# Two transformer layers with routed experts on one core: the order in which group two's shared expert, the layer-1 weights, gathers, sends and the mixing are issued

## The chip, the core and the metric

The kernel runs on one core of a Trainium2 chip. The metric is device time in microseconds (us) of that core. The kernel before was timed in three runs, and its median is what a change is compared with. One further execution was profiled; its times are those of every line of profile in this document.

## What is computed

The input is 8 sequences of 256 tokens with 256 channels, in 32-bit floats. Four blocks follow each other, each on a layer-normed copy of x and each added to x:

```
x = x + attention0(norm(x))      # q, k and v from one projection; softmax over rows plus softmax over columns
x = x + ffn0(norm(x))            # 4 experts, top 2 of them, plus one shared expert for every token
x = x + mixing1(norm(x))         # time mixing: a recurrence over the tokens of a sequence
x = x + ffn1(norm(x))            # 8 experts, top 2 of them
```

ffn0 runs, for every token, silu(x·w1)·(x·w3)·w2 of its two best experts, weighted with their softmax probabilities, and the same form with the shared weights sw1, sw3, sw2. mixing1 projects three mixtures of each token and the one before it to k, v and r, runs an exponentially decaying weighted mean of v with stabilised exponents, layer-norms it, gates it with r and projects it back. ffn1 computes silu-like gates with biases, a product, and a second projection with a bias.

## The kernel before, in words

The sequences are called b0 to b7 here. A sequence lies on the chip as one tile `xs[b]` of 128 partitions by 2 by 256. They are split into two groups, b0 to b4 and b5 to b7 (`GROUPS`, L32). Each group passes each feed-forward block as one `Experts` object (L673): `one` and `two` are the groups of ffn0, `three` and `four` those of ffn1. Such an object works in steps that are Python generators:

- `choose` and `route` (L729, L755): some 35 small VectorE operations that pick two experts per token and give each token two slots in a list that is sorted by expert and padded to blocks of 128 rows.
- `sends` (L806): GpSimd writes the normed rows into a DRAM list `sent` with indirect DMAs, 128 rows each: 20 for a group of five sequences, 12 for a group of three.
- `tiles` (L869): for each block of 128 rows, SyncE's queue fetches the rows (`xg`, L884) and for layer 1 the expert's bias (L883). TensorE turns them (L891), multiplies (L899), turns the hidden values (L891 on `h`) and multiplies again. SyncE stores the result in `back` (L929). There are 23, 15, 27 and 19 tiles in `one`, `two`, `three` and `four`. A fetch waits for every send of its group.
- `shared` (L826): for layer 0 the shared expert of each sequence (matmuls L855, a product on VectorE L860, matmuls L863, an addition to x L866). For layer 1 it adds only the experts' second biases, by the small matmuls L844 and L848.
- `combine` (L948): for each sequence four indirect gathers from `back` on GpSimd (L957), and then four VectorE operations that add them to x (L965).

The time mixing (L980) has ten stages for a sequence, which come in steps of a generator, several sequences at once and four steps apart (`steps`, L1133): norm, mix (transposes L218 of `xr`, then VectorE L1019), project (24 matmul pieces, L1030), exponents, denominator, invert (L1077), numerator, norm_inner (transposes L1096), gate (transposes of `z`, then VectorE L1120) and project_out (L1127). Then come the layer-1 norm (`xm`), its transposes and the router's matmuls (L720). The mixing of b5 starts 8 steps late, since it needs x after `two.combine`.

The order on each engine is made in two layers. By hand, `weave` (L41) interleaves the generators in the given proportions, and `issue_after` ties tile steps behind matmuls of the mixing (`behind`, L1263). A list scheduler then orders the instructions of each engine by priority; a block under `high_priority(offset=...)` (L1151) stands ahead of its place in the program by that many instructions, as far as its inputs allow. Engines run their own queue in order. An instruction that waits holds up all behind it on that engine, on SyncE's and GpSimd's DMA queues too.

The layer-1 weights (`weights_1`, L1191: 24 loads of 256 KB on SyncE's queue) are given the memory that layer 0's weights and tile buffers occupied, so their loads wait for the last matmul that reads these. In the kernel before that is the last L863 of `two.shared`.

The order around the change is: `two.tiles` and then `two.shared` together with the mixing; `three.sends` with the last of them; `two.combine`; then the weights, `three.shared`, and `three.tiles` with the rest of the mixing; then `four`.

Of the kernel before, what the change touches and what calls it, by code (L numbers as in the profile page):

```python
# [12 lines left out]
ALU = mybir.AluOpType  # L13
# [11 lines left out]
E2, I2 = 8, 256  # L25
# [15 lines left out]
def weave(*streams):  # L41

    streams = [[g, n, 0] for g, n in streams]
    while streams:
        s = min(streams, key=lambda s: s[2] / s[1])
        s[2] += 1
        try:
            next(s[0])
        except StopIteration:
            streams.remove(s)  # L50


def one_by_one(*gens):
    for g in gens:
        yield from g


def take(gen, n):
    for _ in range(n):
        try:  # L60
            next(gen)
        except StopIteration:
            return
        yield
# [3 lines left out]
def two_layers(  # L68
# [26 lines left out]
    nc = tc.nc  # L95
# [10 lines left out]
    back = [dram.tile([n, D], F32, tag=f"back{k}", name=f"back{k}") for k, n in enumerate(slots_of)]  # L106
# [566 lines left out]
    class Experts:  # L673
# [195 lines left out]
        def tiles(self):  # L869

            mp, ps, mm, n_tiles, whose = self.mp, self.tile_ps, self.mm, self.n_tiles, self.whose
            xgs, xgTs, hs, hTs, experts, biases = {}, {}, {}, {}, {}, {}

            def fetch(j):
                xgs[j] = mp.tile([P, D], F32, tag="xg", name="xg", bufs=4)
                if self.layer:
                    e = nc.sync.value_load(whose[0:1, j : j + 1], min_val=0, max_val=self.n_experts - 1)  # L880
                    biases[j] = mp.tile([P, 2 * I2], F32, tag="bias", name="bias", bufs=4)
                    row = self.weights[2][ds(e, 1)].rearrange("e g d -> (e g d)")
                    nc.sync.dma_start(out=biases[j], in_=row.partition_broadcast(P))  # L883
                inst = nc.sync.dma_start(out=xgs[j], in_=self.sent[ts(j, P), :]).ins  # L884
                for name in self.senders:
                    tc.add_manual_dep(inst, name, landed, reason="any send may have rows of the tile")

            def flip(src, n, tag):
                pt = ps([P, n, P])
                for c in range(n):  # L890
                    nc.tensor.transpose(pt[:, c, :], src[:, ts(c, P)], ident)  # L891
                to = mp.tile([P, n, P], F32, tag=tag, name=tag)
                nc.scalar.copy(to, pt)  # L893
                return to

            def times(lhsT, w, e, n, cols):
                po = mm([P, cols])
                for c in range(n):
                    nc.tensor.matmul(  # L899
                        po.unsqueeze(1), lhsT=lhsT[:, c, :], rhs=w[:, ds(e, 1), c, :], start=(c == 0), stop=(c == n - 1)  # L900
                    )
                return po

            def up(j):
                at = whose[0:1, j : j + 1]
                e = experts[j] = nc.tensor.value_load(at, min_val=0, max_val=self.n_experts - 1)
                xgT = xgTs.pop(j)
                if self.layer:
                    ph = times(xgT, self.weights[0], e, NC, 2 * I2)
                    hb = mp.tile([P, 2 * I2], F32, tag="hb", name="hb")  # L910
                    nc.vector.tensor_tensor(hb, ph, biases.pop(j), ALU.add)  # L911
                    s = hs[j] = mp.tile([P, I2], F32, tag="h", name="h", bufs=3)
                    nc.scalar.activation(s, hb[:, 0:I2], AF.Silu, scale=ALPHA)
                    (nc.vector if self.last else nc.gpsimd).tensor_tensor(s, s, hb[:, I2:], ALU.mult)  # L914
                else:
                    pu = times(xgT, self.weights[0], e, NC, H1)
                    s = hs[j] = mp.tile([P, H1], F32, tag="h", name="h", bufs=3)
                    nc.scalar.activation(s, pu, AF.Silu)
                    pg = times(xgT, self.weights[2], e, NC, H1)
                    nc.vector.tensor_tensor(s, s, pg, ALU.mult)  # L920

            def down(j):
                py = times(hTs.pop(j), self.weights[1], experts.pop(j), n_hidden, D)
                yg = mp.tile([P, D], F32, tag="yg", name="yg", bufs=3)
                if self.layer:
                    nc.vector.tensor_copy(yg, py)
                else:
                    nc.scalar.copy(yg, py)  # L928
                nc.sync.dma_start(out=self.back[ts(j, P), :], in_=yg)  # L929

            n_hidden = (H1, I2)[self.layer] // P
            for j in range(3):
                fetch(j)
            xgTs[0] = flip(xgs.pop(0), NC, "xgT")
            for j in range(n_tiles + 2):
                if j + 3 < n_tiles:
                    fetch(j + 3)
                if j + 1 < n_tiles:
                    xgTs[j + 1] = flip(xgs.pop(j + 1), NC, "xgT")
                if j < n_tiles:  # L940
                    up(j)
                if 1 <= j <= n_tiles:
                    hTs[j - 1] = flip(hs.pop(j - 1), n_hidden, "hT")
                if j >= 2:
                    down(j - 2)
                yield
# [33 lines left out]
    def time_mixing(rp, rp1, wkv_w, ps, on_pe):  # L980
# [152 lines left out]
        def steps(seqs, first, after):  # L1133

            late = {}
            for b in seqs:
                m = after[b]  # L1140
                stages = [norm, mix, project, exponents, denominator, invert, numerator, norm_inner, gate, project_out]
                for k, f in enumerate(stages):
                    late.setdefault(first[b] + k, []).append((-k, f, b))

                for k, f in enumerate((m.norm, m.flip, m.judge)):
                    late.setdefault(first[b] + len(stages) - 1 + k, []).append((1.5 - len(stages) - k, f, b))
                if b == m.seqs[-1]:
                    late[first[b] + len(stages) + 1].append((1, lambda b, m=m: (m.choose(), m.route()), b))
            for n in range(max(late) + 1):

                with tc.high_priority(offset=3000):  # L1151
                    for _, f, b in sorted(late.get(n, []), key=lambda x: x[0]):
                        f(b)
                yield
# [45 lines left out]
    def layers(is_bounded):  # L1200
# [4 lines left out]
        with ExitStack() as pctx, ExitStack() as ctx0, ExitStack() as actx:  # L1205
# [14 lines left out]
            one, two = (Experts(0, k, w0, lnp, mp, rt, ps, mm, ps) for k in range(2))  # L1220
            group_of = {b: m for m in (one, two) for b in m.seqs}
            with ExitStack() as p1:
                psum.update(pool=p1.enter_context(tc.tile_pool(name="p1", bufs=1, space=PSUM)), ps=4, sc=4)
                if is_bounded:
# [3 lines left out]
                    steps = attention_bounded(ap1, ap2, ep, lambda: (ps, sc))  # L1228
# [20 lines left out]
            yp = pctx.enter_context(tc.tile_pool(name="y", bufs=2))  # L1249
# [7 lines left out]
            three, four = (Experts(1, k, None, lnp, None, rt, sc, mm, ps) for k in range(2))  # L1257
# [3 lines left out]
            mixing = time_mixing(rp, rw, wkv_w, sc, on_pe)(range(B), first, group_of)  # L1261

            def behind(gen, lag=1):  # L1263

                while True:
                    with tc.issue_after(on_pe[-lag].ins):
                        try:
                            next(gen)
                        except StopIteration:
                            return  # L1270
                    yield

            tiles = one_by_one(two.tiles(), two.shared())
            back = one.combine(yp)
            weave((take(back, 2), 2), (take(tiles, 1), 1))
            weave((back, 4), (take(mixing, 3), 3), (take(tiles, 3), 3))
            weave((take(mixing, 25), 25), (take(behind(tiles), 12), 12))
            assert three.chosen
            weave((three.sends(), 10), (behind(tiles), 4))
            weave((two.combine(yp), 4))  # L1280
            ctx0.close()

            wp = pctx.enter_context(tc.tile_pool(name="w2p", bufs=1, side="right"))
# [1 line left out]
            mp = pctx.enter_context(tc.tile_pool(name="moe1", bufs=2, side="right"))  # L1285
            for m in (three, four):
                m.weights, m.mp = w1_, mp
            weave((three.shared(), 5), (take(mixing, 4), 4))
            tiles = three.tiles()
            weave((take(behind(tiles, 3), 22), 22), (mixing, 16))  # L1290
            assert four.chosen
            weave((four.sends(), 6), (four.shared(), 3), (tiles, 7))
            weave((three.combine(yp), 6), (four.tiles(), 21))
            weave((four.combine(yp), 4))

# [14 lines left out]
    with tc.If(is_flat > 0) as which:  # L1310
        layers(True)
    with which.Else():
        attention_any()
        layers(False)
# [61 lines left out]
```

## Time and profile before

| what | value |
|---|---|
| median of 3 runs | 896.68 us (894.17 to 899.22) |
| the profiled execution | 877.61 us |
| its span, first to last instruction | 875.8 us |
| TensorE matmul busy (PE) | 703.4 us, 80% |
| weight loads (PEld) | 442.8 us, 51% |
| VectorE (DVE) | 452.6 us, 52% |
| ScalarE (ACT) | 362.3 us, 41% |
| GpSimd (POOL) | 235.9 us, 27% |
| mean granted TensorE clock | 0.909 |

In the trace the stages lie so: attention up to about 213 us, `one` from there to 376, the tiles of `two` with the mixing of b0 to b4 up to 558, a passage with few matmuls up to the first layer-1 tile at 641.6, then the tiles of `three` with the mixing of b5 to b7, from 777 those of `four`, and after the last matmul at 850 the last combine and the stores of the output.

How to read the views: a line of the timeline has the start in us, the length in us, engine, source line, operation, output<-inputs, shapes, and in square brackets how long the engine had been idle and who released it. A line of the waits has the total of the waits in us, their number and the longest. A line of the table of stretches has the stretch, its length, TensorE's busy time with its number of instructions, the granted clock as a share of full speed, the busy share of the DMA engines, and GB/s.

### The profile page before, as it was taken

The page shows a single profiled execution, that of the slowest core. Times are in us where ns is not written, and L with a number is a line of the kernel's source. Part 1 is how long each engine was busy: PE and PEld are TensorE (multiplying, and loading weights), DVE is VectorE, ACT ScalarE, POOL GpSimd, SP SyncE. Part 2 cuts the span into 40 slices and gives each one's busy share as a digit, 9 for nine tenths or more (in the row PEclk, how much of TensorE's full clock was granted, in tenths as well). Part 3 has the DMA queues.
Part 4 walks back from the last instruction along what each step waited for, and adds up shares of the span by engine and source line. Part 5 has one row for each costly group of instructions (what it writes and reads, how often), then busy time and mean ns, then how long its engine had stood idle before and what let it go on. Part 6 is the DMA issues. An engine that isn't in the chain of part 4 may idle for free.

```text
span 875.8 us, 11122 instructions
## 1 busy us (share of the span) xinstructions
PE 703.4 (80%) x3248; PEld 442.8 (51%) x3248; DVE 452.6 (52%) x1139; ACT 362.3 (41%) x781; POOL 235.9 (27%) x322
## 2 busy tenths in 40 slices
PE   2699888886999999967888889826767887986970
PEld 1354444444756666635565565714535554543640
DVE  4598876881411011126887666405686662345442
ACT  1486766751223333225656663301457342321320
POOL 3634332345320000045010101374012235235004
PEclk9799998987999999998999899965688999998995
DMA  7940000014111111132000000137502345557623
GB/s 237 337 151 1 1 1 1 1 42 152 55 55 49 49 48 37 43 103 67 25 19 25 15 10 19 55 102 246 169 19 78 97 138 163 164 147 220 185 80 110
DMA packets 62307, 76.94 MB, mean 88 GB/s; under 512 B 8184, under 2 KB 50208, under 8 KB 62240
## 3 DMA queue, kind: packets, MB, share of 16 engines
q1 hardware_dynamic: 54560, 58.76, 21.4%
q0 software_dynamic: 6144, 16.79, 6.1%
q10 hardware_dynamic: 1536, 0.60, 0.3%
q8 instruction: 31, 0.51, 0.2%
q14 instruction: 36, 0.29, 0.1%
HBM read 48.57 MB, written 27.54 MB: 87 GB/s over the span
## 4 chain that ended last, share of the span: by engine, by line
PE 46%; DVE 19%; POOL 15%; ACT 8%; issue 6%; DMA 5%; POOLq 0%; DVEq 0%; SPq 0%; ACTq 0%
PE mm L899 24%; POOL rr L473 4%; POOL y L957 4%; PE ps L891 4%; POOL sent L815 4%; PE sc L1030 4%; DMA y<-back,slot 2%; DVE s L535 2%; POOL rs L189 2%; PE sc L521 2%; DVE den L1077 1%; PE mm L848 1%; PE mm L863 1%; PE sc L1127 1%; PE mm L855 1%
## 5 line engine op out<-in xcount | busy, mean ns | idle before, releaser
L957 POOL DMA_INDIRECT y<-back,slot x64 | 62.4, 975 | 206.8 <-PE mm L899 133.5
L899 PE MATMUL mm<-v1s,xgT 128*128 x184 | 91.8, 616 | 1.7 <-ACT xgT L893 1.7
L920 DVE TENSOR_TENSOR h<-h,mm 128x512 f32<-128x512 f32 x38 | 26.1, 686 | 118.4 <-PE mm L899 118.4
L893 ACT COPY hT<-ps 128x256 f32<-128x256 f32 (+1 forms) x84 | 39.3, 468 | 115.8 <-PE ps L891 115.4
L815 POOL DMA_INDIRECT sent<-xm,slot x64 | 62.4, 975 | 56.5 <-DVE pick L787 38.7
L899 PE MATMUL mm<-w2s,hT 128*128 x304 | 73.5, 383 | 1.5 <-ACT yg L928 1.5
L899 PE MATMUL mm<-w3s,xgT 128*128 x152 | 73.3, 605 | 0.0
L899 PE MATMUL mm<-w1s,xgT 128*128 x152 | 72.3, 597 | 0.9 <-issue 0.6
L534 ACT ACTIVATE e<-sc,minus 128x512 f32<-128x512 f32 x96 | 59.7, 705 | 25.8 <-PE sc L521 25.8
L535 DVE TENSOR_REDUCE s<-e 128x2 f32<-128x512 f32 x96 | 60.2, 676 | 12.3 <-ACT e L534 11.9
L188 POOL TENSOR_TENSOR rs<-mv,eps_ln 128x2 f32<-128x2 f32 x40 | 9.1, 228 | 210.6 <-DVE mv L183 112.0
L473 POOL TENSOR_TENSOR rr<-rr,minus_half 128x32 f32<-128x32 f32 x8 | 43.4, 5427 | 65.4 <-DVE rr L472 65.4
L891 PEld LDWEIGHTS ps<-ident,h 128*128 128x128 f32 x244 | 31.3, 143 | 57.8 <-issue 31.1
L899 PEld LDWEIGHTS mm<-w2s,hT 128*128 128x128 f32 x304 | 55.4, 192 | 8.7 <-ACT yg L928 1.8
L965 DVE SCALAR_TENSOR_TENSOR x<-y,share,x 128x256 f32<-128x256 f32 x64 | 30.1, 481 | 52.6 <-DMA y<-back,slot 52.2
L891 PE MATMUL ps<-ident,h 128*128 128x128 f32 x244 | 42.3, 280 | 18.1 <-DVE h L914 9.9
L521 PE MATMUL sc<-qT,kT 32*128 32x512 f32 x256 | 54.0, 676 | 0.8 <-ACT e L534 0.8
L911 DVE TENSOR_TENSOR hb<-mm,bias 128x512 f32<-128x512 f32 x46 | 31.7, 688 | 43.1 <-PE mm L899 37.7
L1030 PE MATMUL sc<-mix,rw 128*128 128x256 f32 x192 | 52.7, 431 | 1.4 <-DVE mix L1019 1.4
L899 PE MATMUL mm<-v2s,hT 128*128 x184 | 49.8, 397 | 1.4 <-DVE hb L911 0.9
L899 PEld LDWEIGHTS mm<-w3s,xgT 128*128 128x128 f32 x152 | 29.2, 194 | 36.0 <-issue 35.7
L1030 PEld LDWEIGHTS sc<-mix,rw 128*128 128x128 f32 x192 | 40.6, 220 | 10.5 <-DVE mix L1019 4.1
(218 smaller groups left out, 1278.4 us busy)
## 6 DMA issues: line engine op xcount, KB each, us to landing
bias<-b1d SPq DMA_DIRECT2D x46, 256.0 KB, 3.6
xg<-sent SPq DMA_DIRECT2D x84, 128.0 KB, 2.2
back<-yg SPq DMA_DIRECT2D x84, 128.0 KB, 2.0
sent<-zero SPq DMA_DIRECT2D x46, 128.0 KB, 1.9
x<-in_x_dram SPq DMA_DIRECT2D x8, 256.0 KB, 5.1
w1s<-in_w_dram SPq DMA_DIRECT2D x4, 512.0 KB, 8.6
w3s<-in_w_dram SPq DMA_DIRECT2D x4, 512.0 KB, 9.4
w2s<-in_w_dram SPq DMA_DIRECT2D x4, 512.0 KB, 10.3
```

Of the source, the lines that this page charges most:

```text
L473: on_pool["last"] = nc.gpsimd.tensor_tensor(rr, rr, minus_half.rearrange("p (t h) -> p t h", h=NH), ALU.pow)
L521: nc.tensor.matmul(pa, lhsT=q["kT"][rows, u, ts(t, P)], rhs=q["qT"][rows, u], start=True, stop=True)
L534: nc.scalar.activation(e, pa, AF.Exp, bias=minus)
L535: nc.vector.tensor_reduce(q["s"][:, t, h : h + 2], e, AX.X, ALU.add)
L815: inst = nc.gpsimd.indirect_dma_start(out=self.sent, out_offset=self.index(k, t), in_=self.xns[self.seqs[t // TT]][:, t % TT, :], in_offse ...
L891: nc.tensor.transpose(pt[:, c, :], src[:, ts(c, P)], ident)
L893: nc.scalar.copy(to, pt)
L899: nc.tensor.matmul(po.unsqueeze(1), lhsT=lhsT[:, c, :], rhs=w[:, ds(e, 1), c, :], start=(c == 0), stop=(c == n - 1))
L911: nc.vector.tensor_tensor(hb, ph, biases.pop(j), ALU.add)
L957: nc.gpsimd.indirect_dma_start(out=y[:, t, k], out_offset=None, in_=self.back, in_offset=self.index(k, TT * i + t))
L965: nc.vector.scalar_tensor_tensor(xs[b][:, t, :], asked[:, t, k], self.share[:, k, at : at + 1], xs[b][:, t, :], ALU.mult, ALU.add,)
L1030: last = nc.tensor.matmul(po[:, o, :], lhsT=w[:, c, ts(o, P)], rhs=m[:, c, :], start=(c == 0), stop=(c == NC - 1))
```

## The change

It has five parts.

1. `two`'s order: four tile steps, then the three steps of `shared`, then the other 13 tile steps, all in front of the router's choice for `three`. Before, `shared` came behind all tile steps and ran along with `three.sends`.
2. `two.combine` and the load of the layer-1 weights are issued right behind the last tile, ahead of `three.sends`. The sends are woven between the steps of the combine and of the mixing. Seven mixing steps lie here and in `three.shared`, where there were four.
3. The mixing's priority block has an offset of 60 instructions in place of 3000.
4. Tiles 20 to 26 of `three` multiply `h` (L914) on VectorE in place of GpSimd.
5. Smaller proportions: 20 tile steps of `three` with 13 mixing steps (before 22 with 16), and a weight of 9 in place of 7 for the tiles beside `four.sends`.

```diff
@@ tiles, up(j), layer 1
-                    (nc.vector if self.last else nc.gpsimd).tensor_tensor(s, s, hb[:, I2:], ALU.mult)
+                    eng = nc.vector if self.last or j >= 20 else nc.gpsimd
+                    eng.tensor_tensor(s, s, hb[:, I2:], ALU.mult)
@@ time_mixing, steps
-                with tc.high_priority(offset=3000):
+                with tc.high_priority(offset=60):
@@ layers
-            tiles = one_by_one(two.tiles(), two.shared())
+            steps = two.tiles()
+            tiles = one_by_one(take(steps, 4), two.shared(), steps)
             back = one.combine(yp)
             weave((take(back, 2), 2), (take(tiles, 1), 1))
-            weave((back, 4), (take(mixing, 3), 3), (take(tiles, 3), 3))
-            weave((take(mixing, 25), 25), (take(behind(tiles), 12), 12))
-            assert three.chosen
-            weave((three.sends(), 10), (behind(tiles), 4))
-            weave((two.combine(yp), 4))
+            weave((back, 4), (take(mixing, 3), 3), (take(tiles, 6), 6))
+            weave((take(mixing, 24), 24), (behind(tiles), 13))
             ctx0.close()
...
-            weave((three.shared(), 5), (take(mixing, 4), 4))
+            back = two.combine(yp)
+            weave((take(back, 1), 1), (take(mixing, 1), 1))
+            assert three.chosen
+            sends = three.sends()
+            weave((take(back, 1), 1), (take(sends, 2), 2), (take(mixing, 1), 1))
+            weave((back, 2), (take(sends, 4), 4), (take(mixing, 2), 2))
+            weave((sends, 4), (take(mixing, 2), 2))
+            weave((three.shared(), 5), (take(mixing, 2), 2))
             tiles = three.tiles()
-            weave((take(behind(tiles, 3), 22), 22), (mixing, 16))
+            weave((take(behind(tiles, 3), 20), 20), (mixing, 13))
             assert four.chosen
-            weave((four.sends(), 6), (four.shared(), 3), (tiles, 7))
+            weave((four.sends(), 6), (four.shared(), 3), (tiles, 9))
             weave((three.combine(yp), 6), (four.tiles(), 21))
             weave((four.combine(yp), 4))
```

## The prediction

> **What bounds the kernel now.** I read the 40 slices first, then TensorE's busy time by stretch, its waits, and the timelines where a gap showed.
>
> ```profile
> PE   2699888886999999967888889826767887986970
> PEclk9799998987999999998999899965688999998995
> ```
>
> TensorE is the busiest engine, with a hole in slices 26 and 27 (569 to 613 us) and a lower clock in 26 to 28. By stretch (start:end, length, TensorE busy, clock, DMA share, GB/s):
>
> ```profile
> 378.00:557.90 179.90, 148.65 (x611) 0.94 0.11 34
> 557.90:601.00 43.10, 18.62 (x77) 0.71 0.33 107
> 601.00:641.60 40.60, 31.09 (x93) 0.67 0.64 197
> 641.60:711.30 69.70, 57.14 (x231) 0.91 0.24 72
> 711.30:850.10 138.80, 119.68 (x446) 0.96 0.54 164
> ```
>
> The stretches are: `two`'s tiles with the mixing; hole; b5's and b6's mixing; `three`'s tiles to `four`'s choice; rest of the tiles. Idle in them: 31.3, 24.5, 9.5, 12.6 and 19.1 us. TensorE's waits from 370 us on (total, times, longest):
>
> ```profile
> PE mm L863 <- DVE hs L860: 21.0, 3, 19.7
> PE sc L1127 <- DVE num L1120: 10.0, 4, 3.2
> PE ps L891 <- DVE h L914: 9.9, 5, 3.4
> PE ps L891 <- POOL h L914: 7.8, 4, 5.0
> ```
>
> The first wait is the hole, the second the mixing's chain; the others belong to `three.combine` and `four.sends`. The hole on GpSimd, VectorE and TensorE:
>
> ```profile
> 584.64 0.96 POOL L815 DMA_INDIRECT sent<-xm,slot  x1 [0.30 <-issue]
> 585.91 0.99 POOL L957 DMA_INDIRECT y<-back,slot  x1 [0.30 <-issue]
> ```
> ```profile
> 588.78 0.48 DVE L965 SCALAR_TENSOR_TENSOR x<-y,share,x 128x256 f32<-128x256 f32 x1 [17.50 <-DMA y<-back,slot]
> 592.98 0.68 DVE L860 TENSOR_TENSOR hs<-hs,mm 128x512 f32<-128x512 f32 x1
> ```
> ```profile
> 593.72 3.78 PE L863 MATMUL mm<-sw2s,hs 128*128 128x256 f32 x8 [19.71 <-DVE hs L860]
> 607.67 8.35 PE L1030 MATMUL sc<-mix,rw 128*128 128x256 f32 x24
> 641.62 2.05 PE L899 MATMUL mm<-v1s,xgT 128*128 x2
> ```
>
> GpSimd issues 20 sends from 560.52, then 12 gathers, one per 1.26 us. VectorE's queue has adds that need those gathers ahead of the last shared product L860, so TensorE stands 19.7 us. Only then do the weights load (597.5) and does b5's mixing start.
>
> **What the Trainium skill says.** Its page "TensorE: Matmul & The Clock Gate" ("What's actually happening"): a TensorE idle for about 3.4 us falls to half clock until it is busy again. The trace agrees: 24 pieces of L1030 took 8.35 us behind the hole, 5.45 at 403.72. "DMA: Bandwidth & Descriptors" ("Anatomy of one DMA — SWDGE (gpsimd) path"): about 2.0 us plus bytes/436e3, an estimate of 2.3 for 128 KB; sends landed in 2.4. The same page ("Issuing engines are not separate DMA queues"): all issuers share 16 DMA engines, only issue time is saved; the gathers kept 1.25 us per issue while weights loaded. "ScalarE: Activation LUTs" ("What ACT_TABLE_LOAD costs"): 1283 ns plus a drain, about 2.66 us per switch; the trace shows the load, 1.28.
>
> **The change, part by part.** I compare the compiled orders and walk along TensorE. T is the end of `two`'s last tile (before 557.9), S the first L899 on `v1s` (before 641.6).
>
> *Shared expert in front.* One sequence is 16 pieces of L855 in 3.47 us and 8 of L863 in 1.99: 5.46, three 16.4. That stretch has 31.3 us of idle. 9.4 come before b0's first transposes, whose place is unchanged; they stay. The shared matmuls fall between b0's L1030 (403.7) and its transposes L1096 (429.5), where waits of 1.5, 0.3 and 0.9 us stood: 2.8 is filled. It also adds three Silus among the Exps: 0 to three switches at 1.28 to 2.66 us. I take 0 on the path, since L1096 comes 39 us behind L1030 in place of 26; uncovered it is 4 to 8 us.
>
> *Smaller lead.* The same tile work is dealt out differently. Behind b0, 19 us of waits are left: 10.0 at L1127, 4.1 at `z`, 3.0 at `xm`, the rest small. I cost this from both sides. At best all go: −19. At worst each of five sequences gains a wait of 4 us at `z`, L1127 or `xm`: +20. The new order has more tile work between L1096 and `z` (4.3 against 1.3 us for b0), but less between L1127 and `xm` (4.1 against 6.5; `xm` took 7.0 us), and VectorE takes b0's L1120 behind b1's reciprocal of 3.3 us, where it came ahead. Starts of L1030 were 27.4, 26.8 and 29.3 us apart from b1 on (422.7, 450.1, 476.9, 506.2). With the shared work b1's main part comes at 440, and the chain k, pp, exponents, bb, L1120, L1127, x, mix comes to about 30 us per sequence: b2 466, b3 496, b4 526. From b4's L1030, its transposes L1096 take 27 us, `z` 4.5, L1127 2.6, `xm` 5, the last tile 2: T = 567, 9 us later with 16.4 more work. Net fill 7.
>
> *Gathers first, then sends.* `back`'s last store lands and the first gather starts 3.0 us behind the last matmul at the end of the kernel (850.1, 853.1): 570. In GpSimd's new queue 11 gathers (13.9 us at 1.26) and one root (1 us) come first: 585. Then come one gather, 20 sends (26.5) and a root: 612.5. The choice needs 10 us behind T (552 to 560.5, plus the late router matmul): hidden by the gathers; if they were gone it would cost all 10. The last send lands 2.4 later and a fetch takes 2.2: first `xg` at 617. b5's mixing starts at 586, L1030 at 590, so b6's mixture is ready at 614. But TensorE's queue has the first transpose of `xg` ahead of b6's L1030: that starts at 617, takes 8.35 at low clock, then four L848 (4.1) and small transposes: S = 631. Queued behind that transpose are only L1030, L848 and the tiles. Before it was 641.6: 10.6 us gained.
>
> *Weights earlier.* They start near 567 and not 597.5. Before, 24 issues took 18 us, ended at 615.4, and first use was 641.6: they bound nothing. I cost this at nothing; the sends hide it until 617. Uncovered, they would need about 24 us. Lower bound: the gathers lose 2 to 4 us of landing to them. On SyncE's queue the first load now stands ahead of the last `back` store: 0.4 us.
>
> *Tiles with the mixing.* From S the work is the same: 176.8 us busy, 31.7 idle (12.6 + 19.1). Before b7's choice TensorE now has 18 tiles, not 11: more cover, of 12.6 I keep 10. L914 on VectorE takes 0.7 us out of GpSimd's sends for seven tiles; the waits of 0.3, 1.75 and 5.0 us go (7 in 711.3 to 730, whose idle is 7.05). But fewer tiles are left to hide `four.sends`: nine (27 us at 3.02) with 4.4 us of L848. SyncE's fetch for `four` waits for the sends ahead of seven stores of `three`: 7.5 us to the first send, 12 × 1.26, 2.4 landing, 3 for a store: 28 us behind the choice. Tile 23 needs a freed `yg` buffer at 24: +4, bounds 0 and 10. The 9.9 of `three.combine` stay. Idle 31.7 − 2.6 − 7 + 4 = 26: 5.6 gained.
>
> *Tail.* 25.7 us from 850.1 on: unchanged.
>
> Sum: 10.6 + 5.6 = 16.2. The profiled execution is 877.61, 1.8 around its span of 875.8; it would become 861.4. The median of the runs shown, 896.68, is 19.1 above that execution; I carry the same 16.2 us over: 880.5.
>
> **Rivals.**
> - *The holes close better.* The fill takes all 19 us, T = 555, and with fewer pauses the clock stays up for b6's L1030 (−2.9): 27.9 less, 868.8 − 4 from the unneeded `yg` wait: about 864.7. For it: 148.65 busy in 179.9. Against it: the order of TensorE's queue is fixed, and the chain per sequence is hardly shorter.
> - *The hole only moves.* GpSimd still does 32 indirect DMAs at 1.26 = 40 us between choice and tiles, and TensorE still has little to do in it. If T is 575 and the weights slow the sends by 3 us, S is 642; the gain is 5.6 less a full `yg` wait (6 more): 897. For it: sends and gathers together took 43 us before (560.5 to 603.5), and take them again.
> - *Slower: the mixing's chain.* With the lead of 60, VectorE and ScalarE take tile work first, and each sequence's chain is queued behind L920 and tile copies that wait for TensorE. Place: L1120 to L1127 to `xm`, b1 to b4. Price: four intervals. At 34 us per sequence in place of 30, T is 583 and the gain is gone; that is the point from which it decides. At 36, T = 591 and the time is 880.5 + 24 = 904.5. For it: those waits are 10.0 us already, and VectorE is busy 32.8 of 40 us in 440 to 480. Against it: before it was 27 to 29.
> - *The change doesn't do what it says.* The first `xg` and the sends, not the weights, release the tiles; so the early weights bring nothing. That is in the forecast already.
>
> **How the numbers follow.** Forecast (gain 5 to 26 us): 0.60. Holes close better: 0.11. Hole only moves: 0.13. Chain slower: 0.16. About 0.5% (4.5 us) is what a measurement of this kernel can tell from no change. Faster by more: 0.71 (the first two); within: 0.13; slower: 0.16. The range goes from the better closing (864) to 899, 2 us above the moving hole; beyond it lie most of the slow chain, about 0.13, and 0.05 at the low end.
>
> **What would show it.** In the changed profile: T near 567, the first L957 on `back1` 3 us later and the 20 sends behind 11 gathers; weights issued near T; no wait of L863 over 2 us; `xr` of b5 near 586; first `v1s` near 631; L914 on GpSimd never inside `four.sends`; a wait of some 4 us on `yg` behind `four`'s choice; tail of 26 us. I am wrong if starts of L1030 are over 34 us apart between b1 and b4, if the gathers slow to well over 1.3 us beside the weights, or if the wait for `four.sends` is 10 us or more.

## The result, and the profile after

The changed kernel takes 883.05 us (median of 4 runs, 880.82 to 884.03) against 897.37 us (894.17 to 899.22). The ratio is 0.9841, 95% interval 0.9806 to 0.9875: 14.3 us faster, where the forecast was 16.2 us faster. It was run again beside the last experiments: ratio 0.9847 (0.9787 to 0.9908).

In code after line 914 the line numbers of the changed kernel are two higher: L914 is now L916, L957 is L959, L1030 is L1032, L1096 is L1098, L1127 is L1129.

The 40 slices of the changed kernel, TensorE's busy tenths and its granted clock:

```profile
PE   3698888986899999995798998844588898985980
PEclk9699989988899999997899999976599999798995
```

The hole is still there, in slices 26 to 28 (573 to 639 us), and so is the low clock. TensorE by stretch, with the columns as in the prediction (start:end, length, busy, clock, DMA share, GB/s), cut at the end of `two`'s last tile, at b5's projection, at the first L899 on `v1s`, at the choice for `four`, and at the last matmul:

```profile
386.88:580.40 193.52, 165.18 (x676) 0.94 0.10 32
580.40:606.33 25.93, 3.55 (x17) 0.59 1.00 323
606.33:645.02 38.69, 28.20 (x91) 0.66 0.30 103
645.02:732.81 87.79, 75.09 (x317) 0.96 0.35 102
732.81:855.68 122.87, 103.15 (x364) 0.93 0.52 156
```

Idle in them: 28.3, 22.4, 10.5, 12.7 and 19.7 us. The stretch in front has grown by 11.7 us for 16.4 us of moved work (193.5 against 181.8 from the same marker on). The idle in the hole is hardly smaller (22.4 us, before 24.5), but the way from the last tile of `two` to the first L899 on `v1s` now takes 64.6 us in place of 83.7. The tiles behind it have about the idle they had. TensorE's waits from 387 us on:

```profile
PE sc L218 <- ACT xr L207: 24.0, 2, 14.6
...
PE ps L891 <- POOL h L916: 7.0, 4, 3.2
PE sc L1129 <- DVE num L1122: 6.6, 4, 3.7
...
PE ps L891 <- DMA xg<-sent: 5.3, 1, 5.3
...
PE mm L863 <- DVE hs L860: 4.0, 1, 4.0
```

The wait of L863 for 19.7 us is gone; one of 4.0 is left among the tiles. In its place stand two others: 14.6 us for b5's `xr`, and 5.3 us for the first `xg`. L1129's wait (L1127 before) has gone from 10.0 to 6.6. The hole on GpSimd (first gather, first and last send) and on TensorE:

```profile
584.49 1.02 POOL L959 DMA_INDIRECT y<-back,slot  x1 [6.54 <-DMA v1s<-in_v1l_dram]
...
600.45 1.04 POOL L815 DMA_INDIRECT sent<-xm,slot  x1 [0.19 <-DVE nb L175]
...
628.38 1.42 POOL L815 DMA_INDIRECT sent<-xm,slot  x1 [0.30 <-issue]
```
```profile
601.14 1.39 PE L218 MATMUL sc<-ident,xr 128*128 128x128 f32 x4 [14.63 <-ACT xr L207]
606.33 8.28 PE L1032 MATMUL sc<-mix,rw 128*128 128x256 f32 x24 [3.79 <-DVE mix L1021]
...
633.70 0.45 PE L891 MATMUL ps<-ident,xg 128*128 128x128 f32 x1 [5.30 <-DMA xg<-sent]
633.94 8.06 PE L1032 MATMUL sc<-mix,rw 128*128 128x256 f32 x24
...
645.02 1.88 PE L899 MATMUL mm<-v1s,xgT 128*128 x4
```

GpSimd issues twelve gathers and twenty sends almost without a pause, as before, only in another order: eleven gathers, four sends, the last gather, sixteen sends. It takes 45.3 us for them, 40.3 before. b5's projection runs in the middle of that, and b6's stands behind one transpose of `xg`.

**Two executions of the same kernel differ by as much as the change.** Both kernels run the same instructions up to a marker: TensorE's transpose of `vec`, behind `one`'s last tile. (The expectations below call it the end of the attention stage; it lies at the end of `one`.) The kernel before had it at 376.14 us in its first profile; the changed kernel had it at 386.88 and 390.94. TensorE from the start to the marker, in the kernel before and then in the changed kernel's second profile:

```profile
0.00:376.14 376.14, 326.87 (x1789) 0.95 0.22 74
```
```profile
0.00:390.94 390.94, 336.92 (x1790) 0.93 0.22 71
```

The same matmuls took 10 us more of busy time at a clock of 0.93 instead of 0.95. So I count everything from the marker on, and set two profiles of each kernel beside each other (us behind the marker):

| | before | before, again | after | after, again |
|---|---|---|---|---|
| end of `two`'s last tile | 181.8 | 180.9 | 193.5 | 193.5 |
| first L899 on `v1s` | 265.5 | 271.0 | 258.1 | 257.8 |
| choice for `four` | 335.1 | 340.4 | 345.9 | 343.3 |
| last matmul | 473.9 | 484.4 | 468.8 | 463.1 |
| end | 499.7 | 510.6 | 494.2 | 488.5 |

The choice for `four` comes behind more tiles in the changed kernel, so that row tells nothing by itself. By the means of two, the end comes 13.8 us earlier: 10.3 of them at the first L899 on `v1s`, 2.9 from there to the last matmul, the rest in the tail. Two profiles of one kernel are up to 10.9 us apart, though. From the first L899 to the last matmul it is 208.4 and 213.4 us before and 210.7 and 205.3 after, so that the 2.9 can't be told from nothing; and by the first profiles alone the end comes only 5.5 us earlier.

### The profile page after: what moved, and what is told of

It is laid out like the page before. It is cut to its first block, busy times and chain, and to the rows that moved or that the text cites. A ratio compares the mean times of both kernels' runs of the same rounds, so it can differ in the third digit from the quotient of the medians.

```text
span 881.1 us, 11114 instructions
## 1 busy us (share of the span) xinstructions
PE 712.2 (81%) x3248; PEld 446.1 (51%) x3248; DVE 457.4 (52%) x1146; ACT 366.5 (42%) x785; POOL 232.8 (26%) x315
## 4 chain that ended last, share of the span: by engine, by line
PE 46%; DVE 18%; POOL 13%; ACT 8%; issue 8%; DMA 4%; another core or an unknown queue 2%; POOLq 0%; SPq 0%; DVEq 0%; ACTq 0%
PE mm L899 23%; POOL y L959 4%; POOL rr L473 4%; PE ps L891 4%; PE sc L521 3%; POOL sent L815 3%; PE sc L1032 2%; PE mm L855 2%; DVE den L1079 2%; POOL rs L189 2%; DMA y<-back,slot 2%; PE mm L863 2%; PE ps L552 2%; PE ps L218 2%
## 5 line engine op out<-in xcount | busy, mean ns | idle before, releaser
L959 POOL DMA_INDIRECT y<-back,slot x64 | 62.3, 973 | 240.8 <-PE mm L899 134.9
L899 PE MATMUL mm<-v1s,xgT 128*128 x184 | 92.4, 627 | 0.9 <-issue 0.8
L899 PE MATMUL mm<-w2s,hT 128*128 x304 | 73.8, 381 | 3.0 <-ACT yg L930 3.0
L815 POOL DMA_INDIRECT sent<-xm,slot x64 | 64.6, 1010 | 43.1 <-DVE pick L787 25.2
L899 PE MATMUL mm<-w1s,xgT 128*128 x152 | 72.6, 595 | 0.8 <-issue 0.7
L899 PE MATMUL mm<-w3s,xgT 128*128 x152 | 72.8, 602 | 0.1
L891 PEld LDWEIGHTS ps<-ident,h 128*128 128x128 f32 x244 | 31.7, 144 | 61.0 <-issue 38.4
L899 PEld LDWEIGHTS mm<-w2s,hT 128*128 128x128 f32 x304 | 54.8, 192 | 9.9 <-ACT yg L930 3.5
L521 PE MATMUL sc<-qT,kT 32*128 32x512 f32 x256 | 58.2, 736 | 0.8 <-ACT e L534 0.8
L1032 PE MATMUL sc<-mix,rw 128*128 128x256 f32 x192 | 50.5, 415 | 3.8 <-DVE mix L1021 3.8
L899 PE MATMUL mm<-v2s,hT 128*128 x184 | 51.3, 399 | 0.8 <-ACT hT L893 0.8
L899 PEld LDWEIGHTS mm<-w3s,xgT 128*128 128x128 f32 x152 | 29.3, 196 | 35.7 <-issue 33.9
L899 PEld LDWEIGHTS mm<-v1s,xgT 128*128 128x128 f32 x184 | 33.2, 201 | 27.3 <-issue 26.8
```

What stands on the lines that cost most here:

```text
L521: nc.tensor.matmul(pa, lhsT=q["kT"][rows, u, ts(t, P)], rhs=q["qT"][rows, u], start=True, stop=True)
L815: inst = nc.gpsimd.indirect_dma_start(out=self.sent, out_offset=self.index(k, t), in_=self.xns[self.seqs[t // TT]][:, t % TT, :], in_offse ...
L899: nc.tensor.matmul(po.unsqueeze(1), lhsT=lhsT[:, c, :], rhs=w[:, ds(e, 1), c, :], start=(c == 0), stop=(c == n - 1))
L959: nc.gpsimd.indirect_dma_start(out=y[:, t, k], out_offset=None, in_=self.back, in_offset=self.index(k, TT * i + t))
L1032: last = nc.tensor.matmul(po[:, o, :], lhsT=w[:, c, ts(o, P)], rhs=m[:, c, :], start=(c == 0), stop=(c == NC - 1))
```

## The experiments

Ratios are to the kernel before, timed beside each run, with a 95% interval. A difference of two ratios is given in us of 897, and its interval is the root of the summed squares of both half-widths.

| run | what it is | ratio | interval |
|---|---|---|---|
| c0_before | before, again | 0.9982 | 0.9950 to 1.0014 |
| b1_shared | before + shared expert in front | 1.0094 | 1.0063 to 1.0125 |
| b3_lead60 | before + smaller lead | 0.9874 | 0.9816 to 0.9932 |
| a2_lead3000 | after with the old lead | 0.9994 | 0.9965 to 1.0023 |
| a4_no916 | after with L916 on GpSimd | 0.9785 | 0.9760 to 0.9811 |
| a5_sendsfirst | after, sends before gathers, flawed | 0.9834 | 0.9785 to 0.9884 |
| a9_sends_first | after, sends before gathers, clean | 0.9973 | 0.9940 to 1.0005 |
| a8_behind | after, first tile behind b6's projection | 0.9698 | 0.9649 to 0.9746 |
| a6_wlate | a8's order with late weights | 0.9826 | 0.9754 to 0.9898 |
| a6b_wlate | the same again | 0.9797 | 0.9726 to 0.9868 |
| b10_best | a8 with L916 on GpSimd, earlier root | 0.9796 | 0.9741 to 0.9852 |
| a0_after | after, again | 0.9847 | 0.9787 to 0.9908 |

**c0_before: the kernel before, profiled again.** No edit.

> The kernel before, unchanged, profiled a second time. Its first profiled execution took 877.6 us where its runs had a median near 897; TensorE's marker transpose of vec at the end of the attention stage stood at 376.1 us there and at 386.9 in the changed kernel, though both run the same instructions up to it. If the first profile was an odd execution, the second one lies near 897 with the marker near 387, and the changed kernel's gain sits wholly behind the marker. If the changed kernel really is slower ahead of the marker, the second profile has it at 376 again.

It took 894.9 us of span, with the marker at 384.32. So the first profile, on which the prediction worked, was a lucky one: 8.2 us of its 19 lie ahead of the marker, and the rest behind it. One place behind the marker can be named. ScalarE stood before the last of the three shared Silus although the matmuls that it reads had ended at 583.9; the trace knows no releaser ("remote"):

```profile
607.82 0.60 ACT L859 ACTIVATE hs<-mm 128x512 f32<-128x512 f32 x1 [33.93 <-remote]
```

In the first profile this Silu ran at 572.3, one matmul group behind its input. In the second the hole ended 5.6 us later (b5's projection at 237.1 behind the marker, not 231.5). The profile of b3_lead60, which also has the shared expert in the hole, shows the same wait, for 38.3 us.

**b1_shared: the shared expert in front, alone.**

```diff
@@ before
-            tiles = one_by_one(two.tiles(), two.shared())
+            steps = two.tiles()
+            tiles = one_by_one(take(steps, 4), two.shared(), steps)
...
-            weave((back, 4), (take(mixing, 3), 3), (take(tiles, 3), 3))
-            weave((take(mixing, 25), 25), (take(behind(tiles), 12), 12))
+            weave((back, 4), (take(mixing, 3), 3), (take(tiles, 6), 6))
+            weave((take(mixing, 25), 25), (behind(tiles), 13))
             assert three.chosen
-            weave((three.sends(), 10), (behind(tiles), 4))
+            weave((three.sends(), 10))
```

> The kernel before with one part of the change alone: the second group's shared expert behind the first four steps of its tiles; sends still ahead of gathers, the old lead of 3000, weights where they were. My theory: the shared matmuls (16.4 us) fill only 3 to 7 us of idle in front, so the last tile of the second group ends 9 to 13 us later; behind it the 20 sends and 12 gathers take their 43 us as before, now with nothing beside them, so the end moves by the same: about 907 us. The rival, that this part brings the gain by itself because the wait of L863 for 19.7 us is gone: 892 or less.

It is slower, by 8.4 us (5.7 to 11.2), at the low edge of what I expected. The wait of L863 for 19.7 us is gone here too, and that did not bring a gain. But it did not go the way I expected. The choice for `three` comes at 174.3 us behind the marker (before 179.4), since the mixing keeps its place ahead, and some 33 us of TensorE's work on `two`'s tiles is left behind it, beside the sends. The last tile ends at 221.3, 39.5 us later than before and not 9 to 13; GpSimd stands 20.6 us between the last send and the first gather. 11.7 us of this is one wait for a copy on ScalarE, which itself stood with no releaser in the trace:

```profile
592.63 3.55 PE L899 MATMUL mm<-w2s,hT 128*128 x8 [11.69 <-ACT yg L928]
```

b5's projection starts at 249.1 (before 231.5 and 237.1). How much of the 8.4 us is due to that one wait, and how much to the order, one profile can't tell.

**b3_lead60: the smaller lead, alone.**

```diff
@@ before, time_mixing, steps
-                with tc.high_priority(offset=3000):
+                with tc.high_priority(offset=60):
```

> The kernel before with the smaller lead (offset 60) alone. My theory: the mixing's chain keeps about its length and some 4 us of the 19 us of waits in the stretch of the mixing are filled: about 893 us. The rival, that tile work gets ahead of the chain on VectorE and ScalarE: starts of L1030 over 29 us apart and 901 us or more. A third: the lead is where most of the change's 14 us comes from: 885.

11.3 us faster (6.1 to 16.5): the third theory. I had given this part 4 us. The profile doesn't show where: the last tile of `two` ends at 178.8 behind the marker (before 181.8 and 180.9), and the span ends at 500.7 (499.7 and 510.6).

**a2_lead3000: the changed kernel with the old lead.** The reverse edit.

> The changed kernel with the old lead of 3000, all else kept. My theory: 4 us of fill are lost in the second group's tiles, little elsewhere: about 887 us. If the lead does most of the gain: 895 or more. If it does nothing: 883.

The whole gain is gone. Against the changed kernel it is 13.7 us slower (9.7 to 17.7). One line of its TensorE shows how (a second like it stands at 476.15): under the big lead the transposes of `xm` stand in TensorE's queue at a place where ScalarE has not yet made `xm`, and tiles that could run stand behind them.

```profile
449.60 1.40 PE L218 MATMUL sc<-ident,xm 128*128 128x128 f32 x4 [6.25 <-ACT xm L207]
```

Its waits for `xm` from the marker to the end of `two`'s tiles come to 13.6 us, and in the changed kernel's second profile to 2.2 (total, times, longest):

```profile
PE sc L218 <- ACT xm L207: 13.6, 5, 6.3
```
```profile
PE sc L218 <- ACT xm L207: 2.2, 3, 1.0
```

The last tile of `two` ends 205.8 us behind the marker in place of 193.5: 8.8 us more of idle and 3.5 more of busy time at a lower clock (0.92 against 0.94). Behind it b6's projection starts at 263.4 in place of 247.1, here behind the first tiles of `three`. In b1_shared, where the old lead and the shared expert in front meet too, the waits for `xm` up to the same point are 12.7 us; in the kernel before they are 3.0 and in b3_lead60 1.9. So it is the shared expert in front that makes these waits under the old lead, and for the kernel before they don't explain what the lead is worth.

**a4_no916: L916 on GpSimd again for all of `three`.**

```diff
@@ after
-                    eng = nc.vector if self.last or j >= 20 else nc.gpsimd
+                    eng = nc.vector if self.last else nc.gpsimd
```

> The changed kernel with the product of line 916 on GpSimd for all of the third group's tiles again (VectorE only in the last group), all else kept. The prediction put 7 us on this part; the changed kernel's profile still shows one 3 us stall on GpSimd's product inside the last sends. My theory: 883 + 7 = 890. The rival, that VectorE's own load takes most of it back: 883 to 885.

It is not slower; by these runs it is 5.0 us faster (1.1 to 8.9), though with a clock of 0.901 to 0.906 where the changed kernel's first four runs had 0.897 to 0.900. The 7 us did not come, and neither theory holds. In the changed kernel two waits are left in the stretch of `four.sends`, and in this run the second is longer:

```profile
746.56 0.44 PE L891 MATMUL ps<-ident,h 128*128 128x128 f32 x2 [3.15 <-POOL h L916]
...
754.89 0.44 PE L891 MATMUL ps<-ident,h 128*128 128x128 f32 x2 [2.07 <-DVE h L916]
```
```profile
738.19 0.44 PE L891 MATMUL ps<-ident,h 128*128 128x128 f32 x2 [3.16 <-POOL h L916]
...
746.45 0.69 PE L891 MATMUL ps<-ident,h 128*128 128x128 f32 x2 [5.02 <-POOL h L916]
```

What this part does is 3 us of waits: the wait of 5.02 became one of 2.07. The product of tile 19, the last that GpSimd keeps, falls between the sends in both.

**a5_sendsfirst and a9_sends_first: the sends ahead of the gathers again.**

```diff
@@ after, a5_sendsfirst
             back = two.combine(yp)
-            weave((take(back, 1), 1), (take(mixing, 1), 1))
+            weave((take(mixing, 1), 1))
             assert three.chosen
-            sends = three.sends()
-            weave((take(back, 1), 1), (take(sends, 2), 2), (take(mixing, 1), 1))
-            weave((back, 2), (take(sends, 4), 4), (take(mixing, 2), 2))
-            weave((sends, 4), (take(mixing, 2), 2))
+            weave((three.sends(), 10))
+            weave((back, 4), (take(mixing, 3), 3))
+            weave((take(mixing, 2), 2))
```

> The changed kernel with the 20 sends ahead of the 12 gathers again, the fifth sequence's mixing behind the gathers, all else kept (small lead, shared expert in front, early weights). My theory: the mixing of the sixth sequence (b5) starts 26 us later, the first tile could start at 617 but its queue holds the mixing; about 8 us are lost: 891. The rival, that the order of the 32 indirect DMAs does not matter, since GpSimd needs 40 us for them either way: 883.

This run tells nothing of the order. The scheduler put eight gathers first all the same, since the slots were not ready; and the mixing of b5 read its x before the experts' sum was added, so that its projection ran at 585, in the middle of the gathers. The clean form ties the gathers behind the last send (`three.sender`):

```diff
@@ after, a9_sends_first, combine
+                    with tc.issue_after(after()) if after else ExitStack():
                         for t in range(TT):
...
@@ layers
+            back = two.combine(yp, lambda: three.sender)
+            weave((take(mixing, 1), 1))
             assert three.chosen
+            weave((three.sends(), 10))
+            weave((take(back, 2), 2))
+            weave((take(mixing, 1), 1))
+            weave((back, 2), (take(mixing, 2), 2))
+            weave((take(mixing, 2), 2))
```

> The changed kernel with all 20 sends queued ahead of all 12 gathers on GpSimd, and the sixth sequence's mixing behind its gathers; else kept. It is the clean form of a5_sendsfirst, where the planner still put eight gathers in front, and where the sixth sequence's mixing read its input before the layer-0 experts' sum was added, so that its chain did not wait for the gathers. My theory: the mixing of b5 starts some 35 us later while the first tiles start earlier, and 8 to 12 us are lost against the changed kernel: about 893. The rival, that the order does not matter because GpSimd issues the same 32 indirect DMAs: 883.

11.8 us slower than the changed kernel (7.6 to 16.1, with the latter's first ratio). On TensorE the first `xg` and b5's `xr` change places:

```profile
623.50 0.66 PE L892 MATMUL ps<-ident,xg 128*128 128x128 f32 x2 [12.94 <-DMA xg<-sent]
...
636.41 1.39 PE L218 MATMUL sc<-ident,xr 128*128 128x128 f32 x4 [9.72 <-issue]
```

Behind the marker, `xg` comes at 232.7 in place of 246.8, and `xr` at 245.6 in place of 214.3. The mixings of b5 to b7 all lie behind that, and the choice for `four` comes at 358.6 in place of 343.3 to 345.9.

**a8_behind: the first tile of `three` behind the projection of b6.**

```diff
@@ after
-            weave((take(behind(tiles, 3), 20), 20), (mixing, 13))
+            weave((take(behind(tiles), 1), 1))
+            weave((take(behind(tiles, 3), 19), 19), (mixing, 13))
```

> The changed kernel with the third group's first tile step queued behind the projection of b6, so that the wait for the first xg no longer holds L1032 back. b6's mixture is ready at 629.4 us and xg at 633.7 in the changed kernel's profile; L1032 takes 8.1 us and what follows needs xg only behind it. My theory: 4 us gained, 879. The rival, that the first tile then comes later by as much: 883.

12.8 us faster than the changed kernel (7.5 to 18.2), three times what I expected, and 0.970 of the kernel before: the best version of this study, 868.4 us. The projection no longer waits for `xg`:

```profile
622.31 7.78 PE L1032 MATMUL sc<-mix,rw 128*128 128x256 f32 x24
...
631.08 0.44 PE L891 MATMUL ps<-ident,xg 128*128 128x128 f32 x2
...
633.22 1.88 PE L899 MATMUL mm<-v1s,xgT 128*128 x4
```

Behind the marker, the first L899 on `v1s` comes at 251.5 (before this edit 257.8 to 258.1) and the choice for `four` at 336.4 (343.3 to 345.9): 6 and 7 to 9.5 us. The rest of the 12.8 lies behind the choice, where TensorE has the same order in both kernels (117.7 us against 122.9 and 119.8); that I can't explain by the edit.

**a6_wlate and a6b_wlate: the layer-1 weights late.** Every load of `weights_1` gets a dependence on the first send of `three`, and stands behind the sends in the program; the order of `xg` and L1032 is then that of a8_behind, which is the base.

```diff
@@ after, weights_1
+            inst = nc.sync.dma_start(out=o, in_=i).ins
+            tc.add_manual_dep(inst, behind, landed, reason="behind a send")
```

> The changed kernel with the layer-1 weight loads held until the first send has landed (about 20 us later), all else kept, except that the planner then puts the projection of b6 (L1032) ahead of the first xg transpose in TensorE's queue, as in the run a8_behind, which is its base. My theory, that early weights bring nothing because the sends hide them: within 2 us of a8_behind, about 879. The rival, that the tiles wait for the weights: 10 us or more above a8_behind.

> The same kernel as a6_wlate (layer-1 weights held until the first send has landed), in more rounds, since its four runs spread from 862 to 888. My theory, that early weights bring little: 868 to 873, within 5 us of a8_behind, since its profile shows no wait for v1s and b5's projection 3 us earlier. The rival, that early weights are worth some 10 us: 880.

By their ratios both runs are slower than a8_behind: by 11.5 us (3.7 to 19.2) and 8.9 us (1.2 to 16.6). So the rivals are nearer. But a6_wlate's four executions spread over 25 us, and the fastest of them, 862.45 us, is as fast as a8_behind's fastest, 863.12; its ratio is that of the other three. The two executions profiled of this one kernel end 483.5 and 501.8 us behind the marker, a8_behind's at 479.5. The traces show only a part of the difference. From the end of `two`'s tiles to b5's projection, with late weights and then in a8_behind:

```profile
570.13:592.58 22.45, 3.55 (x17) 0.60 0.45 119
```
```profile
574.98:600.85 25.87, 3.55 (x17) 0.59 0.99 319
```

With early weights this way is 3.4 us longer, at a DMA share of 0.99 in place of 0.45. Late weights give it back further on. While they load, ScalarE stands before a small copy, with no releaser that the trace knows, and TensorE's L848 behind it:

```profile
617.94 0.36 ACT L846 COPY combT<-ps 8x256 f32<-8x256 f32 x1 [5.98 <-remote]
```

The first L899 on `v1s` comes 254.7 us behind the marker in a6_wlate, 3.2 later than in a8_behind, and it does not wait for the weights. In a6b_wlate it comes at 261.9: TensorE's first L848 stands 17.0 us there, behind ScalarE, which stood 6.1 and 3.0 us with no releaser. That ScalarE stands because the weights load is not shown, and one thing speaks against it: a8_behind has the same wait, 5.05 us before the last but one of these copies, when the DMA engines are only a quarter busy; TensorE has other work at that moment. So what early weights are worth, and why, stays open.

**b10_best: the pieces put together.** a8_behind, with a4's edit, and with the last four gathers tied behind the root of b5's norm on GpSimd (`issue_after(on_pool["last"].ins)`); the first two steps of the sends are issued a little later.

> A version that takes what helped: the changed kernel with the first tile step behind the projection of b6 (a8_behind), the product of line 916 on GpSimd again (a4_no916), and the last four gathers queued behind the root of b5's norm on GpSimd, which stands behind eleven gathers in the changed kernel. My theory: b5's xr comes 4 to 5 us earlier, and 0 to 4 us of it reach the end: 865. The rival, that the first xg, behind the last send, bounds the start of the tiles: 868, as a8_behind.

The root's place moved b5's projection by 1.5 us (24.3 behind `two`'s tiles in place of 25.9), and the first L899 on `v1s` not at all: 251.3 behind the marker. There the rival was right. But the run as a whole is 8.8 us slower than a8_behind (2.2 to 15.4), all of it behind the choice for `four`, which comes at 336.3 and 336.4: 126.7 us from there to the last matmul in place of 117.7. TensorE's busy time takes 4.0 of these, at a clock of 0.89 in place of 0.93; of the 5.0 of idle, the two waits for L916 beside `four.sends` take 1.6 (6.5 in place of 4.9). So a4 says that L916 on GpSimd is a gain, and this run that it is a loss. Its sign stays open.

**a0_after: the changed kernel again.** No edit.

> The changed kernel itself once more, beside the runs that are compared with it: 883 us or 0.984 of the kernel before, with a profile near its first one (the spread of a second profiled execution behind the marker of the attention's end is what single profiles can't resolve).

Its ratio is 0.9847; its profile is the last column of the table above.

## Why the prediction was right, and where only its sum was

The total was right: 16.2 us forecast, 14.3 measured. By stages it agrees as far as can be told: it gave 10.6 us to the first L899 on `v1s` and 5.6 to the tiles behind it; the means of two profiles are 10.3 and 2.9, the latter inside the spread. But what it said of the parts was right for only some of them, and that their sum came out is in part luck.

- **Shared expert in front.** "Net fill 7" for it and the lead together put T 9 us later; it came 11.7 later, a fill of 4.7. That the part alone is a loss of 9 to 13 us followed from the same sum (16.4 less what it fills), and b1_shared measured 8.4; but its last tile came 39.5 us later, so that the way was another. No wait of L863 over 2 us was forecast; one of 4.0 stands.
- **Smaller lead.** This is the step that failed: the term of the sum for the lead, and with it the one for the shared expert, were mis-sized. The prediction gave the lead about 4 us, from bounds of −19 and +20. It is worth 11.3 us in the kernel before and 13.7 in the changed one, about as much as the whole change. I had costed both parts one at a time, on the waits of the kernel before (3.0 us at `xm`). The runs show that they act on each other. With the old lead, the shared expert in front puts T 24.0 us later (205.8 in a2_lead3000) where the sum has 13.6 (16.4 less 2.8), and the waits for `xm` grow to 13.6 us; the smaller lead takes 12.3 off again (193.5), where the sum has some 4. What I had missed: I looked at the chain of one sequence and asked whether it gets longer, and not at where its matmuls stand in TensorE's queue. There `xm`, under the old lead, stands ahead of tile work that could run. The two errors nearly cancel, so T came 2 to 3 us from its forecast by luck. Why the lead is worth 11.3 us without the shared expert in front, where T moves by only 2 to 3 us, is open. The starts of L1032 from b1 on (445.1, 482.5, 510.6, 536.3) are 30.4 us apart on average, where I had worked out 30. But the first interval is 37.4 us, over the 34 that I had named as a sign of being wrong: b1's 24 pieces are dealt out over 14 us among the tiles. The next two, 28.1 and 25.7, make up for it.
- **Gathers first.** Right, as far as the steps go. The forecast of 10.6 us is what is left at S with T 9 us later, so from T to S it shortens the way by some 20 us, of which the shared expert's absence is a part; measured, the way is 64.6 and 64.3 us after 83.7 and 90.1. The order alone, reversed in a9_sends_first, costs 11.8. Counted from T, the steps were: first gather 3 forecast, 4.1 measured; first send 19 and 20.1; first `xg` 50 and 53.3; b5's projection 23 and 25.9; b6's mixture 47 and 49.0; S 64 and 64.6. That "TensorE's queue has the first transpose of `xg` ahead of b6's L1030" was read from the order; a8_behind shows that this place costs the changed kernel 12.8 us, of which the traces account for 7 to 9.5. b5's projection came 3 us later than forecast, 1.1 of them before the first gather; beside the weights 2 to 4 had been named as a bound and not used.
- **Weights earlier.** Costed at nothing. By the ratio of a6b_wlate they are worth 8.9 us (1.2 to 16.6), by that of a6_wlate 11.5, with executions too far apart to lean on. This is on the base of a8_behind, where the first tile starts earlier; on the changed kernel itself it was not tried. Nothing was perhaps too little, but neither size nor mechanism is shown.
- **Tiles with the mixing.** Idle was to fall from 31.7 to 26; in two profiles of the changed kernel it is 32.4 and 30.6. The 7 us for L914 were not there: it removes 3 us of waits, and its sign in time is open. I had counted on no GpSimd product inside `four.sends`, and tile 19's is there. The wait of some 4 us on `yg` did not come either: when `four`'s tiles start at 778, their `xg` is ready.
- **Tail.** 25.4 us, as forecast (25.7).

The parts measured one at a time don't add up to 14.3: the lead 11 to 14, gathers first 12, weights perhaps 9, the shared expert −8. Each is worth more or less beside the others: with the old lead the four other parts together bring nothing (a2_lead3000, 0.9994). My reading is that they share one resource, the time in which TensorE's queue has something ready; only for the lead and the shared expert is that shown.

The rivals: that the hole only moves (897) and that the chain is slower (904.5) are refuted by the time. That early weights bring nothing is open, as said. "The holes close better" did not happen: T is at 193.5 behind the marker, where 179 was needed (555 less 376.1). a8_behind comes near its number (868.4 against 864.7), but by another way, with T at 193.3. That number doesn't come out of its own terms either: 16.2, 12 for T at 555 in place of 567, and 2.9 make 31.1, not 27.9, and with the 4 of the `yg` wait 861.6.

## What to carry to other kernels

Before costing a priority, ask where it puts instructions in the in-order queue of the engine that bounds the kernel, not only whether it makes the favoured chain longer: an instruction that stands there before its input is ready holds up all ready work behind it (6.25 us for one `xm` here). A part costed alone on the old kernel can be worth something else beside the other parts. Read the compiled order at both edges of a hole; here one 128-row transpose in front of a projection cost 7 to 13 us, where the whole change gained 14. And take a second profile of the same kernel before subtracting stages: a total that fits can be made of steps that don't.

## What was not expected of the hardware

- The same program spreads by 2% from execution to execution. The kernel before ran from 885.6 to 902.3 us in 55 runs on one chip, with granted clocks from 0.891 to 0.915. The stage of identical instructions ahead of the marker took 376 to 391 us in fourteen profiles, at 0.95 down to 0.92.
- ScalarE and VectorE stood at times for 5 to 15 us, and twice, each time before the last shared Silu (L859), for 33.9 and 38.3, and the trace knew no releaser. In c0_before the matmuls that this Silu reads had ended 24 us before, as the trace has them. The first profile of the kernel before has no such wait, the second has eight of them. What they are is open.
- The Trainium skill's page "TensorE: Matmul & The Clock Gate" ("What's actually happening") has the clock come back after at least one busy window of about 3.4 us. The traces agree: behind the hole it came back after 5.8 us of work in the changed kernel, 5.2 in its second profile, 5.9 in the kernel before. Of the 24 pieces of L1032 the first 14 ran at half clock and the rest at full, so that they took 8.28 us in place of 5.45. TensorE in three stretches of the changed kernel:

```profile
606.33:612.12 5.79, 5.79 (x14) 0.50 0.69 253
612.12:618.95 6.83, 3.36 (x20) 1.00 0.23 78
620.67:628.42 7.75, 7.73 (x18) 0.50 0.24 85
```

Not the hole alone, then, makes the mean clock of 0.66 up to the first layer-1 tile. TensorE stood again, 5.2 us before the first L848 and 5.3 before `xg`, and the clock was at half from 618.95 to 639.43. In between it was busy for 7.7 us without a break with L848 and L844, and stayed at half (third line; 7.7 us in the second profile too, and 9.8 in b1_shared). L848 multiplies with 8 rows in place of 128. Whether such small matmuls count as idleness for the clock was not tested.
